# The opening of a graph layer and attention kernel: two elements' first products placed together, with loads and VectorE's order rearranged

## The chip, the cores and the metric

The kernel runs on one NeuronCore of one Trainium2 chip. The metric is device time in microseconds (us). A NeuronCore has TensorE (PE in the profile; PEld is its weight load), VectorE (DVE), ScalarE (ACT), GpSimd (POOL) and SyncE (SP), whose queue here issues the transfers between the chip's large memory (HBM) and the on-chip memory (SBUF). Products of TensorE land in a third memory, PSUM, of which this kernel uses eight banks of 128 x 512 numbers.

## The reference

The input x has 64 elements of 256 x 512 numbers (256 graph nodes with 512 features); adj is one 256 x 256 graph of zeros and ones. All arithmetic is in 32-bit floats. Two layers follow each other, each with a residual addition and a layer normalization over the features:

```python
a = adj.astype(x.dtype)
deg = a.sum(axis=1)
mi, mj = x @ Wi.T, x @ Wj.T                      # W = [Wi | Wj], 512 x 1024
h = layernorm(x + deg * (mi + b) + a @ mj)       # per element, layer 0
q, k, v = h @ Wq.T + bq, h @ Wk.T + bk, h @ Wv.T + bv   # 8 heads of 64
p = softmax(where(adj == 0, -inf, q @ k.T / 8))
out = layernorm(h + (p @ v) @ Wo.T + bo)         # layer 1
```

## The kernel before

The elements are worked through in pairs, 32 passes. In the steady loop (line 982 on) layer 0 of the next pair is woven between the attention of the present pair. Before the loop stands an opening, written out by hand, which brings the weights and the first two elements in, runs layer 0 for both, and then the first projections.

Layer 0 of an element takes seven block products instead of eight, with sums of blocks on both sides. `xB` is a loaded element, in an order that VectorE turns by one transpose into `xT` (`turn_x`, line 488). The left sums `S1` to `S4` of `xT` go to `xS` (`sum_x`, line 494). On the weights' side `w0` holds seven blocks: three come straight from memory (B11 and B21 of Wi, B22 of Wj), and T1 to T4 are made from them by `combine` (line 923), where T3's place first receives the raw B12 of Wj. Steps 1 to 7 of `l0_steps` (line 502) are the products, each two matmuls of 128 x 128 by 128 x 512:

- step1 is x times B11, into the bank "x"; ScalarE copies it out as the keeper `u1`. step3 adds x times B21 to the same bank.
- step2 is x times T4, into the bank "w"; the result goes, scaled by the degree, into the residual `xh`.
- step4 (S2 with T2) and step6 (S3 with T3) share the bank "y"; after step4 VectorE writes the keeper `u2` = y + `u1`, after step6 `u3` = y + `u1`.
- step5 (S1 with T1) and step7 (S4 with B22) share the bank "z". `mj`'s second half is z after step5 plus `u3` (added on GpSimd); its first half is z after step7 plus `u2`.
- each half of `mj` is split into `hi` (ScalarE) and `lo` (GpSimd). Step 8, `neighbours`, multiplies the graph with both. Steps 9 to 14 normalize the rows (`take`, `give`) and, in the loop, send them on.

In the lists `p` (element 0) and `q` (element 1) these steps are counted from 0: `p[0]` is step1, `p[7]` is `neighbours`, `p[12]` is the normalization of the first row block.

What sets the order. A planner in the language places the instructions and all waits. TensorE's instructions, and those of other engines that are wrapped in `in_order` (line 282), are pinned behind the instruction that was written before them on the same engine. The others may move when their inputs are there. SyncE issues transfers in the order of the profile's issue lines. A tile of a pool has as many buffers as the pool says per tag: the banks of layer 0 and of the projections (`bank`, tag "mm") are three, the value bank (`value_bank`) is one, the keepers (tag "lu") are three, and tiles in `p1` have one. A tile that finds no buffer waits until an earlier one has been read for the last time.

In the opening before, SyncE issues the first x, then B11, the raw B12, adj, B21, B22, the first residual and the biases; the second x follows when the transpose of the first has freed its only buffer. The products are run in the order of lines 940 and 945, then `make_factors` (line 412) makes right-hand sums of the attention weights, `h_transpose` turns element 0's rows for the projections, and line 962 starts these.

Of the kernel before, what the change touches and what calls it, by code (L numbers as in the profile page):

```python
# [8 lines left out]
F32 = mybir.dt.float32  # L9
# [7 lines left out]
P = 128  # L17
# [201 lines left out]
B11, B21, B22, T1, T2, T3, T4 = range(7)  # L219
# [5 lines left out]
def unshifted_path(ctx, tc, flag, x, adj, wiT, wjT, b0, wqT, bq, wkT, bk, wvT, bv, woT, bo, out):  # L225
# [16 lines left out]
    nc = tc.nc  # L242
    B, N, D = x.shape
# [3 lines left out]
    R = 32  # L247
# [9 lines left out]
    p1 = ctx.enter_context(tc.tile_pool(name="p1", bufs=1))  # L257
# [11 lines left out]
    def bank(name):  # L269
        return ps_m.tile([P, 512], F32, tag="mm", name=name)  # L270
# [27 lines left out]
    def load_x(b):  # L298
        if b < B:
            xh[b] = p6.tile([P, NT, D], F32, tag="xh", name="xh")  # L300
            nc.sync.dma_start(out=xh[b], in_=x[b].rearrange("(t p) d -> p t d", p=P))

    b_bc = p4.tile([P, D], F32, tag="u", name="b_bc")
    xB, hB = {}, {}

    def load_xB(b):
        if b < B:
            xB[b] = p1.tile([P, N // R, P], F32, tag="xB", name="xB")
            for q in range(D // P):
                nc.sync.dma_start(out=xB[b][q * R:(q + 1) * R],  # L310
                                  in_=x[b][:, q * P:(q + 1) * P].rearrange("(r a) n -> r a n", r=R))

    load_xB(0)
    w0 = const.tile([P, 7, 2, D], F32, name="w0")
    adj_i = p2.tile([P, NT, N], I32, tag="pe", name="adj_i")
    for n, w, h in ((B11, wiT, 0), (T3, wjT, 0), (None, None, 0), (B21, wiT, 1), (B22, wjT, 1)):
        if n is None:
            nc.sync.dma_start(out=adj_i, in_=adj.rearrange("(t p) j -> p t j", p=P))
        else:
            nc.sync.dma_start(out=w0[:, n], in_=w.rearrange("(p h c) o -> p h c o", h=2, c=2)[:, h])  # L320
    load_x(0)
    nc.sync.dma_start(out=b_bc, in_=b0.to_broadcast([P, D]))

    xT, xS, hT, hS, qT, kT, vv, aoT, oS = ({} for _ in range(9))

# [20 lines left out]
    def degrees():  # L346
        in_order(nc.vector.tensor_copy(a, adj_i))
        in_order(nc.vector.tensor_reduce(deg, a, AX.X, ALU.add))

    def turn_graph():  # L350
        for t in range(NT):
            pt = score_bank("pt_a")[:, :N]
            for i in range(NT):
                transpose(pt[:, i * P:(i + 1) * P], a[:, i, t * P:(t + 1) * P], ident)

            in_order(nc.vector.tensor_copy(graph[:, t, :], pt))
            in_order(nc.scalar.copy(aT[:, t, :], pt))
# [28 lines left out]
    def bias_steps():  # L386
        for t, d in ((bq_sb, bqd), (bk_sb, bkd)):
            in_order(nc.vector.tensor_sub(d, t[:, 2:4], t[:, 0:2]))
# [83 lines left out]
    def left_blocks(a11, a12, a21, a22, s):  # L472
        return {"A11": a11, "A12": a12, "A21": a21, "A22": a22,
                "S1": s[:, 0], "S2": s[:, 1], "S3": s[:, 2], "S4": s[:, 3]}
# [13 lines left out]
    def turn_x(b, tag="xT"):  # L488
        if b < B:
            xT[b] = p1.tile([P, NC, N], F32, tag=tag, name="xT")  # L490
            transposed(xT[b], xB.pop(b))
            load_xB(b + 1)

    def sum_x(b):
        if b < B:
            a11, a12, a21, a22 = (xT[b][:, 2 * k:2 * k + 2, t * P:(t + 1) * P]
                                  for t in range(NT) for k in range(2))
            xS[b] = left_blocks(a11, a12, a21, a22, p1.tile([P, 4, 2, P], F32, tag="xS", name="xS"))
            for step in left_steps(xS[b], in_order):
                step()  # L500

    def l0_steps(b):
        banks, k = {}, {}

        def product(name, left, n, first):
            if first:
                banks[name] = bank("po")
            for c in range(2):
                matmul(banks[name], left[:, c, :], w0[:, n, c, :], start=(first and c == 0),
                                 stop=(c == 1), skip_group_check=True)  # L510

        def raw(t, h):
            return xT[b][:, 2 * h:2 * h + 2, t * P:(t + 1) * P]

        def keeper(name):
            k[name] = p3.tile([P, D], F32, tag="lu", name=name)
            return k[name]

        def add_scaled(t, src):
            nc.vector.scalar_tensor_tensor(xh[b][:, t, :], src, deg[:, t:t + 1], xh[b][:, t, :],  # L520
                                           ALU.mult, ALU.add)

        def split(t):
            nc.scalar.copy(k["hi"][:, t, :], k["mj"][:, t, :])
            nc.gpsimd.tensor_tensor(k["lo"][:, t, :], k["mj"][:, t, :], k["hi"][:, t, :].bitcast(F32),
                                    ALU.subtract)

        def step1():
            product("x", raw(0, 0), B11, True)
            nc.scalar.copy(keeper("u1"), banks["x"])  # L530

        def step2():
            product("w", raw(1, 1), T4, True)
            add_scaled(1, banks["w"])

        def step3():
            product("x", raw(0, 1), B21, False)
            add_scaled(0, banks["x"])

        def step4():  # L540
            product("y", xS[b]["S2"], T2, True)
            nc.vector.tensor_add(keeper("u2"), banks["y"], k["u1"])

        def step5():
            product("z", xS[b]["S1"], T1, True)
            k["mj"] = p1.tile([P, NT, D], F32, tag="mj", name="mj")
            nc.scalar.copy(k["mj"][:, 1, :], banks["z"])  # L547

        def step6():
            product("y", xS[b]["S3"], T3, False)  # L550
            nc.vector.tensor_add(keeper("u3"), banks["y"], k["u1"])
            nc.gpsimd.tensor_tensor(k["mj"][:, 1, :], k["mj"][:, 1, :], k["u3"], ALU.add)

            k["hi"] = p1.tile([P, NT, D], F32R, tag="hi", name="hi")
            k["lo"] = p1.tile([P, NT, D], F32R, tag="lo", name="lo")
            split(1)
            add_scaled(1, k["u3"])

        def step7():
            product("z", xS[b]["S4"], B22, False)  # L560
            nc.vector.tensor_add(k["mj"][:, 0, :], banks["z"], k["u2"])
            split(0)

        stats = {}

        def neighbours():
            k["pa"] = score_banks("pa")
            for i in (1, 0):
                for n, (j, part) in enumerate((j, part) for j in (1, 0) for part in ("hi", "lo")):
                    matmul(k["pa"][:, i, :], graph[:, j, i * P:(i + 1) * P], k[part][:, j, :],  # L570
                           start=(n == 0), stop=(n == 2 * NT - 1))

        def take(t):
            r = xh[b][:, t, :]
            in_order(nc.vector.tensor_add(r, k["pa"][:, t, :], r))
            stats[t] = norm_stats(r, in_order)

        def give(t):
            norm_apply(xh[b][:, t, :], *stats[t], in_order)


        return [step1, step2, step3, step4, step5, step6, step7, neighbours, lambda: take(1), lambda: take(0),
                lambda: give(1), lambda: send_h(b, 1), lambda: give(0), lambda: send_h(b, 0)]
# [30 lines left out]
    def h_transpose(b, t, borrow=False):  # L614

        g, i = divmod(b, NB)
        if i == 0 and t == 1:
            new_h(g)
        pt = (score_banks("pt_h")[:, 0, :] if borrow else bank("pt_h")).rearrange("p (c n) -> p c n", c=NC)
        for c in range(NC):  # L620
            transpose(pt[:, c, :], xh[b][:, t, :].rearrange("p (n c) -> p c n", c=NC)[:, c, :], ident)
        nc.scalar.copy(hT[g][:, :, i * N + t * P:i * N + (t + 1) * P], pt)
        if t == 0 and i == NB - 1:
            sum_h(g)
# [284 lines left out]
    def run(steps):  # L909
        for s in steps:  # L910
            s()
# [12 lines left out]
        in_order(nc.vector.tensor_sub(w0[:, n], w0[:, m], w0[:, k]))  # L924

    turn_x(0)
    load_x(1)
    raw_q, raw_k = load_raw(wqT, "kT"), load_raw(wkT, "oS")
    load_x(2)
    raw_v, raw_o = load_raw(wvT, "v"), load_raw(woT, "aoT")  # L930
    for _ in range(6):
        bring()
    sum_x(0)
    combine(T1, T3, B11)
    degrees()
    combine(T2, B22, T1)
    combine(T4, B21, T2)
    combine(T3, B22, T3)
    p, q = l0_steps(0), l0_steps(1)
    run([p[0], p[2], p[4], p[3]])  # L940
    turn_x(1, "hB")
    degree_bias()
    add_bias(0)
    turn_graph()
    run([p[1], p[5], q[0], p[6], q[2]])
    add_bias(1)
    sum_x(1)
    run(q[1:2] + p[7:11] + q[3:5] + p[12:13])
    make_factors(wqT, "wq", raw_q)
    for _ in range(AHEAD - 6):  # L950
        bring()
    bias_steps()
    h_transpose(0, 1)
    run(q[5:6])
    h_transpose(0, 0)
    run(q[6:7])
    make_factors(wkT, "wk", raw_k)
    o = second_late(qk_steps(0, qT, "qT", bq_sb, bqd, True))
    k = second_late(qk_steps(0, kT, "kT", bk_sb, bkd, True))
# [22 lines left out]
    for g in range(NG - 1):  # L982
# [15 lines left out]
        w = NB * NC - 2  # L998
# [3 lines left out]
        o = o_steps(g)  # L1002
# [111 lines left out]
```

## Time and profile before

| | us |
|---|---|
| median of 4 runs | 3116.52 |
| lowest and highest | 3114.95 and 3118.49 |
| the profiled execution | 3119.08 |
| its span, first to last instruction | 3117.2 |
| TensorE busy in the span | 3073.8 |
| VectorE busy | 2148.9 |
| GpSimd busy | 1521.8 |
| ScalarE busy | 1008.3 |

A row of the profile gives a source line, an engine, an operation with the tile that it writes and the ones that it reads, their shapes, a count and durations. In the timeline a row begins with the start and the length in us; the brackets at its end give how long the engine had been idle and what ended the wait. One matmul of 32-bit floats is recorded as two, so that a product of layer 0 is four records. Line 290 is the helper through which all matmuls go; the tile names tell them apart: `po` from `w` and `xT` or `xS` is layer 0, `pa` the neighbours, `pt_h` a transpose of rows, `st` a projection. SPq is SyncE's issuing queue. A DMA issue line gives the KB of one and the us from issue to landing.

### The profile page before, as it was taken

Reading aid. Unit: us, or ns where it says so; the run is one execution under the profiler, and the core shown is the slowest. Engines: PE = TensorE matmul, PEld = TensorE weight load, DVE = VectorE, ACT = ScalarE, POOL = GpSimd, SP = SyncE. Lnnn points to the kernel's source line nnn. Section 1 sums busy time; section 2 is a strip of 40 time slices with the busy share of each in tenths; the row PEclk is TensorE's granted clock in tenths of the full one; section 3 lists DMA queues with packets and bytes.
Section 4 is the critical chain, followed back from the end, with each engine's and each line's share of the span. In section 5 each row is a group of like instructions: output and inputs, shape, how many; then the busy total and the mean of one; then the engine's idle time right before and its main releaser. Section 6 shows DMA issues by size and latency. Waiting matters only on the chain. (4 is left out here: it accounts for less than half of the span.)

```text
span 3117.2 us, 42777 instructions
## 1 busy us (share of the span) xinstructions
PE 3073.8 (99%) x14598; PEld 2118.4 (68%) x14598; DVE 2148.9 (69%) x3234; ACT 1008.3 (32%) x1925; POOL 1521.8 (49%) x1255
## 2 busy tenths in 40 slices
PE   7999999999999999999999999999999999999998
PEld 4667766677666777666776667766677766677665
DVE  6766676766677666676667676667766767767665
ACT  2332333323333333333233333333333333323332
POOL 2544545544545445464454544455544546445453
PEclk9999999999999999999999999999999999999999
DMA  7355534455444554445553445544455444555333
GB/s 245 123 151 157 166 118 133 132 157 165 140 123 126 155 168 149 117 128 154 158 157 123 132 136 157 165 136 125 127 154 169 145 120 126 155 162 160 116 113 96
DMA packets 410395, 447.28 MB, mean 143 GB/s; under 512 B 40896, under 2 KB 300224, under 8 KB 409792
## 3 DMA queue, kind: packets, MB, share of 16 engines
q1 hardware_dynamic: 410176, 444.50, 48.1%
q8 instruction: 120, 1.97, 0.3%
q14 instruction: 99, 0.81, 0.1%
HBM read 340.79 MB, written 70.25 MB: 132 GB/s over the span
## 5 line engine op out<-in xcount | busy, mean ns | idle before, releaser
L461 POOL TENSOR_TENSOR rstd<-ve,mhalf 128x1 f32<-128x1 f32 x256 | 140.8, 555 | 725.9 <-DVE below L459 725.9
L812 POOL TENSOR_TENSOR pk<-pe 128x512 f32<-128x512 f32 x256 | 322.2, 1275 | 340.7 <-ACT pe L809 340.6
L290 PE MATMUL po<-w,xS 128*128 128x512 f32 x1024 | 470.9, 602 | 6.1 <-ACT mj L547 5.7
L290 PE MATMUL st<-hS,factor 128*128 128x256 f32 x2048 | 452.7, 379 | 1.2 <-DVE u L685 1.2
L290 PEld LDWEIGHTS st<-hS,factor 128*128 128x128 f32 x2048 | 388.2, 190 | 55.3 <-DVE u L685 1.6
L809 ACT ACTIVATE pe<-pe 128x1024 f32<-128x1024 f32 x256 | 270.8, 1058 | 379.2 <-DVE pe L805 379.2
L290 PE MATMUL st<-hT,factor 128*128 128x256 f32 x1536 | 360.7, 381 | 9.1 <-ACT u L711 8.4
L290 PE MATMUL po<-w,xT 128*128 128x512 f32 x768 | 354.3, 604 | 14.7 <-DVE xS L478 9.4
L290 PEld LDWEIGHTS po<-w,xS 128*128 128x128 f32 x1024 | 187.2, 190 | 253.0 <-issue 191.6
L290 PEld LDWEIGHTS st<-hT,factor 128*128 128x128 f32 x1536 | 289.0, 190 | 61.6 <-ACT u L711 20.9
L805 DVE TENSOR_TENSOR pe<-ps,maskT 128x1024 f32<-128x1024 f32 x256 | 297.8, 1194 | 35.2 <-PE ps L290 35.2
L882 DVE RECIPROCAL rden<-den 128x256 f32<-128x256 f32 x127 | 222.9, 1755 | 74.0 <-PE den L290 68.5
L290 PEld LDWEIGHTS po<-w,xT 128*128 128x128 f32 x768 | 144.2, 192 | 183.1 <-issue 163.6
L290 PE MATMUL ps<-qT,kT 64*128 64x256 f32 x2048 | 264.9, 392 | 0.0
L883 POOL TENSOR_TENSOR rtot<-rtot,rden 128x256 f32<-128x256 f32 x127 | 92.7, 730 | 330.1 <-DVE rden L882 330.1
L290 PE MATMUL pav<-pe,v_sb 128*64 128x256 f32 x2048 | 250.1, 386 | 1.9 <-ACT pe L809 1.8
L740 DVE TENSOR_TENSOR xh<-st,xh 128x512 f32<-128x512 f32 x186 | 144.6, 777 | 151.5 <-PE st L290 151.5
L290 PEld LDWEIGHTS pav<-pe,v_sb 128*64 128x64 f32 x2048 | 135.2, 136 | 154.1 <-issue 71.9
L290 PEld LDWEIGHTS ps<-qT,kT 64*128 64x128 f32 x2048 | 184.3, 186 | 78.2 <-issue 51.3
L290 PE MATMUL st<-factor,hS 128*128 128x256 f32 x1024 | 234.8, 382 | 0.0
L290 PE MATMUL st<-factor,oS 128*128 128x256 f32 x992 | 224.2, 379 | 0.0
L290 PEld LDWEIGHTS st<-factor,hS 128*128 128x128 f32 x1024 | 191.9, 190 | 35.4 <-issue 10.6
(115 smaller groups left out, 4658.2 us busy)
## 6 DMA issues: line engine op xcount, KB each, us to landing
xB<-in_x_dram SPq DMA_DIRECT2D x256, 128.0 KB, 3.7
xh<-in_x_dram SPq DMA_DIRECT2D x64, 512.0 KB, 4.5
factor<-wq SPq DMA_DIRECT2D x128, 256.0 KB, 4.3
factor<-wk SPq DMA_DIRECT2D x128, 256.0 KB, 2.6
factor<-wv SPq DMA_DIRECT2D x128, 256.0 KB, 2.6
spread<-rden SPq DMA_DIRECT2D x1016, 32.0 KB, 1.9
factor<-wo SPq DMA_DIRECT2D x124, 256.0 KB, 3.1
h_cols<-xh SPq DMA_DIRECT2D x124, 256.0 KB, 2.4
```

The lines of the kernel that those rows point to most:

```text
L290: in_order(nc.tensor.matmul(*args, **kw))
L461: nc.gpsimd.tensor_tensor(rstd, ve, mhalf, ALU.pow)
L740: nc.vector.tensor_add(dst, src, dst)
L805: nc.vector.tensor_add(pe.rearrange("p j t q -> p j (t q)"), ps.rearrange("p j t q -> p j (t q)"), maskT.rearrange("p t q -> p (t q)").uns ...
L809: in_order(nc.scalar.activation(flat, flat, AF.Exp, scale=QSCALE, accum_out=etot[:, NB * g + i, pr:pr + 1]))
L812: nc.gpsimd.tensor_tensor(pk, pe[:, :, 0, :], pe[:, :, 1, :], ALU.add)
L882: nc.vector.reciprocal(rden, den)
L883: nc.gpsimd.tensor_tensor(rtot, rtot, rden, ALU.add)
```

## The change

The second element's x is loaded at the start, into the buffer tagged "hS", which is idle in the opening, and the other loads are put in another order: B11, B21, the second x, adj, the raw B12, B22, the bias, the two residuals. The third x is issued right behind the second transpose in the program, ahead of the raw attention weights. VectorE sums the first x right after its transpose, then turns the second, and only then takes the graph and combines the weights. The sums of the second x go to the buffer tagged "qT" instead of "xS", so that they need not wait for the first's. TensorE runs the two products by B11 and B21 of element 0, then those of element 1, and then the products by combined weights; element 1's bank "x" is the value bank. The second bias addition is placed after element 0's statistics, and each `h_transpose` stands behind a product of element 1 instead of before it.

```diff
-    def load_xB(b):
+    def load_xB(b, tag="xB"):
         if b < B:
-            xB[b] = p1.tile([P, N // R, P], F32, tag="xB", name="xB")
+            xB[b] = p1.tile([P, N // R, P], F32, tag=tag, name="xB")
...
-    for n, w, h in ((B11, wiT, 0), (T3, wjT, 0), (None, None, 0), (B21, wiT, 1), (B22, wjT, 1)):
-        if n is None:
-            nc.sync.dma_start(out=adj_i, in_=adj.rearrange("(t p) j -> p t j", p=P))
-        else:
-            nc.sync.dma_start(out=w0[:, n], in_=w.rearrange("(p h c) o -> p h c o", h=2, c=2)[:, h])
+    def load_w0(n, w, h):
+        nc.sync.dma_start(out=w0[:, n], in_=w.rearrange("(p h c) o -> p h c o", h=2, c=2)[:, h])
+
+    load_w0(B11, wiT, 0)
+    load_w0(B21, wiT, 1)
+    load_xB(1, "hS")
+    nc.sync.dma_start(out=adj_i, in_=adj.rearrange("(t p) j -> p t j", p=P))
+    load_w0(T3, wjT, 0)
+    load_w0(B22, wjT, 1)
+    nc.sync.dma_start(out=b_bc, in_=b0.to_broadcast([P, D]))
     load_x(0)
-    nc.sync.dma_start(out=b_bc, in_=b0.to_broadcast([P, D]))
+    load_x(1)
...
             transposed(xT[b], xB.pop(b))
-            load_xB(b + 1)
-
-    def sum_x(b):
+            if b > 0:
+                load_xB(b + 1)
+
+    def sum_x(b, tag="xS"):
...
-    def l0_steps(b):
+    def l0_steps(b, bank_of_x=bank):
...
             if first:
-                banks[name] = bank("po")
+                banks[name] = (bank_of_x if name == "x" else bank)("po")
...
     turn_x(0)
-    load_x(1)
+    sum_x(0)
+    turn_x(1, "hB")
     raw_q, raw_k = load_raw(wqT, "kT"), load_raw(wkT, "oS")
     load_x(2)
     raw_v, raw_o = load_raw(wvT, "v"), load_raw(woT, "aoT")
     for _ in range(6):
         bring()
-    sum_x(0)
+    degrees()
     combine(T1, T3, B11)
-    degrees()
     combine(T2, B22, T1)
     combine(T4, B21, T2)
     combine(T3, B22, T3)
-    p, q = l0_steps(0), l0_steps(1)
-    run([p[0], p[2], p[4], p[3]])
-    turn_x(1, "hB")
+    p, q = l0_steps(0), l0_steps(1, value_bank)
+    run([p[0], p[2], q[0], q[2], p[4], p[3]])
+    turn_graph()
+    sum_x(1, "qT")
     degree_bias()
     add_bias(0)
-    turn_graph()
-    run([p[1], p[5], q[0], p[6], q[2]])
+    run([p[1], p[5], p[6], q[1], q[3]])
+    run(p[7:11] + [q[4]])
     add_bias(1)
-    sum_x(1)
-    run(q[1:2] + p[7:11] + q[3:5] + p[12:13])
+    run([p[12]])
     make_factors(wqT, "wq", raw_q)
     for _ in range(AHEAD - 6):
         bring()
     bias_steps()
+    run(q[5:6])
     h_transpose(0, 1)
-    run(q[5:6])
+    run(q[6:7])
     h_transpose(0, 0)
-    run(q[6:7])
     make_factors(wkT, "wk", raw_k)
```

More of the change, by code (lines that the diff above doesn't have):

```diff
@@ L497, in sum_x @@
                                   for t in range(NT) for k in range(2))
-            xS[b] = left_blocks(a11, a12, a21, a22, p1.tile([P, 4, 2, P], F32, tag="xS", name="xS"))
+            xS[b] = left_blocks(a11, a12, a21, a22, p1.tile([P, 4, 2, P], F32, tag=tag, name="xS"))
             for step in left_steps(xS[b], in_order):
                 step()
-    def l0_steps(b):
+    def l0_steps(b, bank_of_x=bank):
         banks, k = {}, {}
```

## The prediction

> **What bounds the kernel now.** I read the page first, then busy time by stretch, TensorE's timeline of the opening, the granted clock, the load issues with their time to landing, and the waits of SyncE's queue.
>
> ```profile
> PE 3073.8 (99%) x14598; PEld 2118.4 (68%) x14598; DVE 2148.9 (69%) x3234; ACT 1008.3 (32%) x1925; POOL 1521.8 (49%) x1255
> ```
>
> TensorE (PE) is busy nearly throughout: 43.4 us idle in 3117.2. By stretch (PE is the number after the length):
>
> ```profile
> 0.00:60.00 60.00, 43.71 (x120) 23.29 (x121) 37.73 (x59) 13.13 (x25) 16.06 (x20) 0.97 0.80 261
> ...
> 130.00:3000.00 2870.00, 2856.36 (x13634) 1979.40 (x13632) 1986.41 (x2985) 938.54 (x1794) 1420.35 (x1165) 1.00 0.48 143
> ```
>
> So 16.3 of the idle lie in the first 60 us, where the change is; 13.6 are spread over the middle. What TensorE saves before its first attention product therefore reaches the end, if nothing late takes its place. Its opening (start, length, then in brackets the idle time before):
>
> ```profile
> 9.38 3.75 PE L290 MATMUL po<-w,xT 128*128 128x512 f32 x4 [9.38 <-DVE xS L478]
> 14.45 3.75 PE L290 MATMUL po<-w,xT 128*128 128x512 f32 x4 [1.32 <-DMA w<-in_wiT_dram]
> ...
> 28.50 3.57 PE L290 MATMUL po<-w,xT 128*128 128x512 f32 x4 [2.77 <-DVE xT L485]
> ...
> 39.64 3.70 PE L290 MATMUL po<-w,xS 128*128 128x512 f32 x8 [0.44 <-DVE xS L478]
> 44.51 0.75 PE L293 MATMUL pt_h<-ident,xh 128*128 128x128 f32 x4 [1.17 <-ACT xh L467]
> ...
> 48.18 0.75 PE L293 MATMUL pt_h<-ident,xh 128*128 128x128 f32 x4 [1.21 <-ACT xh L467]
> ...
> 50.49 1.89 PE L290 MATMUL st<-hT,factor 128*128 128x256 f32 x8
> ```
>
> A product of layer 0 is four records. Up to about 18.5 they start 0.86 apart (3.44 a product), later 0.43 (1.72): half clock, though the clock column has no record before 18.5. Halved again here:
>
> ```profile
> 28.80:32.10 3.30, 3.30 (x5) 1.24 (x4) 2.04 (x3) 0.70 (x2) 2.94 (x2) 0.50 1.03 423
> ```
>
> Ledger of 9.38 to 50.49, 41.1 us: idle 1.32 + 2.77 + 0.44 + 1.17 + 1.21 = 6.9; half clock over 3.75 + 4.05 (14.45 to 18.5) + 3.4 = 11.2 busy us, of which half, 5.6, is loss; work at full clock 28.6. Avoidable at most: 12.5. The start at 9.38 is B11's landing (issued 3.47, 5.8 later), not the VectorE line that the view names. Loads, by issue, with time to landing:
>
> ```profile
> w<-in_wiT_dram SPq DMA_DIRECT2D x1, 512.0 KB, 5.8
> ...
> w<-in_wjT_dram SPq DMA_DIRECT2D x1, 512.0 KB, 8.2
> ...
> adj_i<-in_adj_dram SPq DMA_DIRECT2D x1, 256.0 KB, 8.4
> ...
> w<-in_wiT_dram SPq DMA_DIRECT2D x1, 512.0 KB, 9.3
> ```
>
> They land at 9.3, 12.3, 13.0, 14.4. SyncE also stalls:
>
> ```profile
> SPq L392 <- DMA w<-in_wjT_dram: 2.4, 1, 2.4
> ...
> SPq L310 <- DMA w<-in_wiT_dram: 1.0, 1, 1.0
> ```
>
> In both the issue waits for the load eight places ahead: eight are in flight at most.
>
> **What the Trainium skill says.** "TensorE: Matmul & The Clock Gate", Part 1: the clock starts at half and is granted after a busy window of 3.4 us, windows running freely. The trace agrees: changes at 18.5, 28.8, 32.2. "PSUM — Partial Sum Buffer", PSUM bank collisions: two engines may not use one bank at once, so a copy out must finish before the next matmul into it; no run here shows a collision. "SBUF — State Buffer", Who interferes with whom: VectorE and GpSimd share a port pair under an exclusive lock. The trace agrees: a sum (L478) took 2.50 us beside a GpSimd bias addition, 0.42 elsewhere.
>
> **The change, part by part.** p and q are the steps of elements 0 and 1, numbered from 0.
>
> Loads. B11 stays second, so PE starts at 9.4 again. B21 takes T3's place: 12.3. Then by bytes at the 364 GB/s of 9.4 to 15.1 us (0.5 MB in 1.44): second x 13.8, adj 14.5, T3 16.0, B22 17.4, b0 18.1, xh0 19.5, xh1 21.0. The second x is in rows of 512 B, costlier: 13.3 to 15.5. The eight-deep limit costs nothing there: B22's issue waits for B11 (9.3), the bias for B21 (12.3), when earlier loads are still moving. xB2's four issues now stand before the raw weights on SyncE; the last waits for xh1, about 21, against 20.3 for the first raw weight now. Then 0.5 MB more goes ahead: raw weights 2 to 3 us later, the first factor at about 38 instead of 36.4, needed at 45. Hidden by 7 us; without that cover, 2.
>
> VectorE. Second transpose 13.8 to 15.9 (2.06); adjacency cast and degrees 1.11: 17.0; T1, T2, T4, T3 at 1.21 each: 18.2, 19.4, 20.7, 21.9. They are wanted on PE at about 20.8, 22.5, 24.8, 26.5. Hidden, with 2.5 us spare.
>
> PE. Removed: 1.32, 2.77, 0.44, 1.17, 1.21 and the second half-clock stretch. The last two waits go because two second-element products and a finished normalization now stand between. Added:
> - p0 to p2 share a bank, and the copy u1 (0.59, 13.17 to 13.76) must come between: 0.70. Today B21's landing hides it. B21 at 12.3 is in time.
> - q0 to q2 likewise; today p6 lies between. 0.59, hand-over 0.1, and 0.17 of overlap lost: 0.87.
> - The keepers "lu" have three buffers. q's u1 takes one early; u1 and u2 of p hold the others. p's u3 (p5) must wait until u2 is released, by the addition behind p6. PSUM follows: q1's bank is the fourth of three. The x bank of p has passed to p1, whose addition into xh0 waits for the first bias addition (GpSimd, 2.35, not over before 31). So q1 waits for the addition behind p6: 0.95 (bounds 0 and 1.5).
> - u3 late makes GpSimd late: bias addition to about 31.6, then 1.28 for mj, 0.62 on ScalarE, 1.27 each for two lo parts: 35.5. PE reaches the neighbours' product at 34.2: 1.3 (bounds 0 and 2.5).
> - The last transpose now stands directly before the first q product: the copy of hT (0.59) is bare, 0.75. Today a product of 1.88 covers it.
>
> Sum of idle 4.6. Half clock: from 9.38 with a gap of 0.7; if the window ending at 15.1 counts as busy, 5.05 us at half, loss 2.5; if not, until 18.5, 8.4 us, loss 4.2. (Today's window there, 62% busy, did not count; this one would be 80%.) New total 7.1 or 8.8 against 12.5: saving 5.4 or 3.7, 4.6 in the middle. The steps after 50 keep their order: unchanged. xh1's bias addition is moved behind the statistics of element 0 on GpSimd; behind it waits only q5's addition into xh1: nothing.
>
> Against the profiled execution (3119.1; span 3117.2, 1.9 around it) this gives 3114.5. That execution lies 2.6 above the median; the second half-clock stretch (1.7) needs a window that catches most of the 2.77 idle, and I estimate that a run in four or two lacks it. Against the median, 3116.5, I take 4.2: **3112.3**.
>
> **The rivals.**
> *Fuller gain* (0.20): neither the slot nor GpSimd is late: 0.95 + 1.3 more, 3110, with the clock early 3108.5. For it: GpSimd is 16 us busy in 60. Against: u3's buffer is counted, not estimated.
> *Late loads eat it* (0.15): second x after 16. VectorE's whole order stands behind its transpose; each us is one of PE and keeps the clock low. 3 us late gives about 3116. For it: slow rows of 512 B. Against: the first x, with the same rows, was in use at 6.4.
> *Slower* (0.13): the remaining order is planned afresh, and in each of the 31 later passes one wait grows, most likely VectorE behind GpSimd's lock. Today a pass idles 13.6/31 = 0.44 us. From 0.14 us a pass the gain is gone, from 0.35 it is slower by over 0.2%: at 0.4, 3124.7. For it: 2.50 for 0.42 shows what one lock costs. Against: PE's order is written out, and at 69% VectorE has room.
> That the change does not do what it says: a small part of the second rival.
>
> **How the numbers follow.** The forecast has 0.52, its own range 3110 to 3115. 0.2% is 6.2 us, about what a measurement of this kernel can tell from no change: 3110.3 and 3122.7 are the borders. Faster: most of the fuller gain and a small part of the forecast, 0.25. Slower: 0.15, the rival and some of what I have not seen. Same: 0.60. Range for 8 in 10: 3108 to 3118, which takes in the fuller gain and late loads and leaves out the slower case.
>
> **What would show it.** First product at 9.4; B21's product 0.7 after u1's copy; second transpose over by 16.5; q0 without a wait; u3 of p after the addition behind p6; a wait of about 1 before q1 and of about 1 before the neighbours' product; first q product at 44 to 46 instead of 50.49; middle idle 13 to 14 us. Wrong if the second x lands after 16, if the clock stays half beyond 18.5, or if the middle's idle moves by over 4.

## The result, and the profile after

The changed kernel has a median of 3119.66 us against 3116.92 for the kernel before: 2.7 us more. The measured ratio is 1.0011 with a 95% interval of 1.0006 to 1.0016 (the medians alone give 1.0009). That is inside the 0.2% of the forecast "same", but it lies on the other side of no change than the 3112.3 that was predicted, and outside the range of 3108 to 3118. The profiled execution took 3118.74 us.

What lies after the opening did not change. Busy time by stretch, changed kernel (start and end, length, then busy time of each engine, PE first):

```profile
0.00:60.00 60.00, 42.84 (x122) 23.31 (x123) 39.89 (x60) 13.00 (x25) 17.05 (x20) 0.97 0.82 264
...
130.00:3000.00 2870.00, 2856.54 (x13636) 1979.67 (x13630) 1986.87 (x2986) 938.71 (x1794) 1420.38 (x1164) 1.00 0.48 143
```

The middle idles 13.5 us, as before (13.6), so what changed lies in the opening. This execution took 0.3 us less than the profiled one of the kernel before (3119.08), although the median is 2.7 more: that one was slow in its opening, as its second execution shows further down. Its waits can be compared line by line; its total can't stand for the median. The opening on TensorE, changed kernel:

```profile
8.39 3.71 PE L290 MATMUL po<-w,xT 128*128 128x512 f32 x4 [8.39 <-DVE xS L482]
12.77 1.98 PE L290 MATMUL po<-w,xT 128*128 128x512 f32 x4 [0.68 <-ACT u L536]
15.21 1.98 PE L290 MATMUL po<-w,xT 128*128 128x512 f32 x4 [0.45 <-DVE xT L490]
17.87 1.98 PE L290 MATMUL po<-w,xT 128*128 128x512 f32 x4 [0.68 <-ACT u L536]
...
30.27 1.98 PE L290 MATMUL po<-w,xT 128*128 128x512 f32 x4 [1.40 <-DVE xh L526]
32.09 1.88 PE L290 MATMUL po<-w,xS 128*128 128x512 f32 x4
35.19 0.49 PE L290 MATMUL pa<-hi,graph 128*128 128x512 f32 x1 [1.22 <-ACT hi L530]
36.54 0.50 PE L290 MATMUL pa<-lo,graph 128*128 128x512 f32 x1 [0.85 <-POOL lo L531]
...
42.15 0.75 PE L293 MATMUL pt_h<-ident,xh 128*128 128x128 f32 x4 [0.29 <-ACT xh L472]
...
44.46 0.68 PE L293 MATMUL pt_h<-ident,xh 128*128 128x128 f32 x4
48.34 7.13 PE L290 MATMUL st<-hT,factor 128*128 128x256 f32 x24 [3.21 <-ACT hT L628]
```

Of the five waits that were to go, the one for B21, the one for element 1's sums and the one before the last transpose are gone; 0.45 of the 2.77 for the second transpose of x is left (none in a second execution, below), and 0.29 of the 1.17 before the first transpose of rows. The last transpose starts at 44.46, when nothing but the first q product is left to start; before, that product started at 50.49 (47.40 in the second execution). Then TensorE stands still for 3.21 us until ScalarE has copied the transposed rows, and the clock is taken down behind the wait:

```profile
49.60:52.80 3.20, 3.20 (x9) 2.57 (x8) 3.17 (x5) 1.36 (x3) 1.29 (x1) 0.50 0.90 273
```

That costs about another 1.7 us: the eight records of the q product that start from 49.58 to 52.57 are 0.43 apart, the others 0.22. Why the copy is late can be read from two queues. ScalarE, changed kernel:

```profile
44.24 0.56 ACT L628 COPY hT<-pt_h 128x512 f32<-128x512 f32 x1
47.19 0.62 ACT L530 CAST hi<-mj 128x512 fp32r<-128x512 f32 x1 [2.38 <-POOL mj L558]
47.71 0.58 ACT L628 COPY hT<-pt_h 128x512 f32<-128x512 f32 x1
```

The second copy of hT stands behind `hi` of element 1, and `hi` waits 2.38 us for GpSimd's `mj`. GpSimd, changed kernel:

```profile
42.16 0.99 POOL L466 TENSOR_TENSOR rstd<-ve,mhalf 128x1 f32<-128x1 f32 x1 [1.24 <-DVE below L464]
43.13 2.36 POOL L379 TENSOR_TENSOR xh<-xh,degb 128x1024 f32<-128x1024 f32 x1
45.44 1.71 POOL L558 TENSOR_TENSOR mj<-mj,u 128x512 f32<-128x512 f32 x1
```

The second bias addition (L379) stands behind element 0's statistics, where the change put it. It takes 2.36 us, and `mj` waits behind it. The chain of the loss is then: bias addition, `mj`, `hi`, copy of hT, first q product. (VectorE's sums for the weights, 0.68 alone, took 2.77 and 1.74 beside these two GpSimd instructions. VectorE is not in this chain: the keeper that `mj` adds was written by 43.34.)

### The profile page after: what moved, and what is told of

Read it like the earlier page. It is cut to its first block, busy times and chain, and to the rows that moved or that the text cites. A ratio compares the mean times of both kernels' runs of the same rounds, so it can differ in the third digit from the quotient of the medians.

```text
span 3116.8 us, 42774 instructions
## 1 busy us (share of the span) xinstructions
PE 3072.6 (99%) x14598; PEld 2118.2 (68%) x14598; DVE 2151.0 (69%) x3234; ACT 1008.1 (32%) x1925; POOL 1522.5 (49%) x1255
## 5 line engine op out<-in xcount | busy, mean ns | idle before, releaser
L290 PE MATMUL po<-w,xT 128*128 128x512 f32 x768 | 351.3, 600 | 12.8 <-DVE xS L482 8.4
```

Of the source, the lines that this page charges most:

```text
L290: in_order(nc.tensor.matmul(*args, **kw))
```

## The experiments

Theory A: this chain is the loss, and the added place of the bias addition is its cause. Theory B: the loss lies elsewhere, in the loads, the clock at the start or the shared banks. All medians below are compared with the kernel before on the same chip (3117.0 in the first group, 3116.2 in the second, 3117.1 in the third), and "over before" is the difference; brackets give the ratio and its 95% interval.

**The bias addition earlier, or later.** In the traces of both, the order on VectorE and ScalarE is that of the changed kernel, as far as operations and tile names tell; on GpSimd one instruction stands elsewhere.

```diff
     run([p[1], p[5], p[6], q[1], q[3]])
+    add_bias(1)                       # bias_early
     run(p[7:11] + [q[4]])
-    add_bias(1)
...
     h_transpose(0, 0)
+    add_bias(1)                       # bias_late, instead
```

> Changed kernel, with the second bias addition moved ahead of element 0's statistics; only GpSimd's order differs. Theory A (the addition stands before element 1's mj on GpSimd, so hi is late, and hi stands before the last copy of hT on ScalarE): the wait before the first q product falls from 3.2 to under 1 us and the clock is not lowered behind it, so 2.3 + 1.7 = 4 us less than the changed kernel, 3115.7, ratio to before 0.9996. Theory B (the loss lies elsewhere, in loads or in the clock at the start): within 1 us of the changed kernel, 3119 to 3120.

> Changed kernel, with the second bias addition moved behind element 1's last layer-0 product. Theory A: as with the early place, about 4 us less than the changed kernel, 3115.7; GpSimd then adds the bias after both lo parts, when nothing waits for it. Theory B: 3119 to 3120.

Measured: 3116.94 (0.1 under before, ratio 1.0, 0.9991 to 1.0008) and 3116.75 (0.3 under before, the same interval). So 2.7 and 2.9 us of the changed kernel go with one instruction's place in a queue, that is, the whole of its loss. (Its interval, from 1.0006, and theirs, to 1.0008, just touch, but two places of the instruction give the same, and the traces show why.) The wait, early place, then ScalarE there:

```profile
47.15 3.72 PE L290 MATMUL st<-hT,factor 128*128 128x256 f32 x16 [1.13 <-ACT hT L628]
```

```profile
45.12 0.56 ACT L628 COPY hT<-pt_h 128x512 f32<-128x512 f32 x1
45.99 0.62 ACT L530 CAST hi<-mj 128x512 fp32r<-128x512 f32 x1 [0.30 <-POOL mj L558]
46.51 0.58 ACT L628 COPY hT<-pt_h 128x512 f32<-128x512 f32 x1
```

And with the late place:

```profile
49.16 3.72 PE L290 MATMUL st<-hT,factor 128*128 128x256 f32 x16 [1.13 <-ACT hT L628]
```

The wait falls from 3.21 to 1.13, and that of `hi` from 2.38 to 0.30. Theory A holds for the loss against the kernel before; B is out, since loads and banks are as in the changed kernel. The gain is smaller than the 4 expected. In the profile of either kernel the clock is lowered after all, now at the neighbours' product (early place, its records 0.43 apart instead of 0.23):

```profile
35.90:39.10 3.20, 3.14 (x7) 2.48 (x8) 0.00 (x0) 0.00 (x0) 2.33 (x2) 0.50 0.81 260
```

The waits there, 1.22 and 0.85, are those of the changed kernel, so the move did not lengthen them. Why the clock falls behind them in one execution and not in another is worked out in the last section.

**The transposes back ahead of element 1's products.** The bias addition stays late; this asks whether ScalarE's order alone can mend it.

```diff
-    run(q[5:6])
     h_transpose(0, 1)
-    run(q[6:7])
+    run(q[5:6])
     h_transpose(0, 0)
+    run(q[6:7])
```

> Changed kernel, with the two transposes of rows put back ahead of element 1's last two products; the bias addition stays late. Theory A: ScalarE copies hT ahead of hi, so the first q product waits for nothing, but the first transpose waits about 2 us for its normalization: first q product at about 46.8 instead of 48.3, and 1.7 of clock, 3 us less, 3116.7. A rival within A (GpSimd alone counts, not ScalarE's order): no gain, 3119 to 3120.

Measured: 3118.62, 1.6 over before (1.0006, 0.9998 to 1.0014). That is about 1 us less than the changed kernel, within the intervals, and 1.9 more than theory A expected. The wait of 3.2 is gone, as theory A says, but the wait that this order has by itself took its place, with a lowered clock (43.8 to 47.0):

```profile
43.70 1.13 PE L293 MATMUL pt_h<-ident,xh 128*128 128x128 f32 x4 [2.01 <-ACT xh L472]
...
49.78 3.40 PE L290 MATMUL st<-hT,factor 128*128 128x256 f32 x15
```

(This execution also waited 1.56 us, until 16.75, for the second transpose of x, against 0.45 in the changed kernel's.) By the waits the change's order of the transposes is the better one once the addition is out of the way: 0.29 and 1.13 us in the kernels above against 2.01 here. The two orders were not run against each other with the addition moved.

**The wait filled with idle matmuls**, to price the clock by itself. The three matmuls are additional, and nothing reads their results.

```diff
     h_transpose(0, 0)
+    spare = score_bank("spare")
+    for _ in range(3):
+        matmul(spare, xT[1][:, 0, 0:P], w0[:, B11, 0, :], start=True, stop=True)
```

> Changed kernel with three more matmuls of 128x128 by 128x512 (2.6 us, into a spare bank, results unused) between the last transpose and the first q product; they fill the wait of 3.2 us. If the lowered clock behind the wait costs 1.7 us: first q product still at 48.3, its matmuls 0.22 apart at once, 3118.0. If the clock costs nothing or the wait doesn't set it: 3119.7 or more.

Measured: 3118.45, 1.4 over before (1.0005, 0.9997 to 1.0014): 1.3 less than the changed kernel by the difference to before, for 1.7 expected. The first q product started at 49.08, 40.0 us after the first product, as in the changed kernel (48.34 and 8.39). In its profile the clock stays full from 12.0 us to the end of the work. The interval reaches to the changed kernel's ratio, so the size is only rough; that the clock is lost behind the wait, and kept when the wait is filled, is what the traces show.

**u3's missing buffer.** The prediction had named it as the cause of the waits at q1 and at the neighbours' product. The second bias addition is in its late place.

```diff
-            k[name] = p3.tile([P, D], F32, tag="lu", name=name)
+            k[name] = p4.tile([P, D], F32, tag="lu", name=name)
...
-        pool, tag = (p3, "lu") if early and name == "u1" else (p4, "u")
+        pool, tag = (p4, "lu") if early and name == "u1" else (p4, "u")
```

> The kernel with the second bias addition moved behind element 1's last product (3116.8), and four keepers of tag lu instead of three. If u3's missing buffer costs what its waits show (1.40 before q1, about 2.1 before and in the neighbours' product, and the lowered clock that they bring): 3 us less, 3113.7, ratio to before 0.9989, no wait before q1. If GpSimd's chain alone sets the neighbours' product: only 1.4 less, 3115.4.

Measured: 3113.32, 2.9 under before (0.999, 0.9981 to 0.9998), 2.7 less than the late bias addition alone by the same measure. No wait before q1, and little in the neighbours' product:

```profile
28.76 1.88 PE L290 MATMUL po<-w,xT 128*128 128x512 f32 x4
...
32.79 0.50 PE L290 MATMUL pa<-lo,graph 128*128 128x512 f32 x1 [0.20 <-POOL lo L531]
...
34.02 0.50 PE L290 MATMUL pa<-lo,graph 128*128 128x512 f32 x1 [0.50 <-POOL lo L531]
```

Of 3.47 us of waits at these two places 0.70 are left, and the clock is full from 13.0 on. The missing buffer is shown as the cause of these waits; how many of the 2.7 us are theirs is rough, since the two intervals overlap.

**The first bias addition later**, with three keepers and the second addition in its late place, since the trace ends q1's wait with the addition into xh0.

```diff
-    add_bias(0)
-    run([p[1], p[5], p[6], q[1], q[3]])
+    run([p[1], p[5], p[6]])
+    add_bias(0)
+    run([q[1], q[3]])
```

> As above with three keepers, but the first bias addition is moved behind element 0's last product in the program, so that on GpSimd and on the bank of p1 nothing waits for it. If q1 waits for that bank (the trace ends the wait with the addition into xh0): no wait before q1, 1.4 less, and some of the wait in the neighbours' product, 3114.6. If u3's buffer is what q1 waits for: no change at q1, 3116.8.

Measured: 3118.10, 1.9 over before (1.0004, 0.9995 to 1.0012), where 3114.6 was expected. The wait before q1 is gone, so the bank of p1 was its nearer cause. But GpSimd now does the addition between `mj` and the second `lo`, and the neighbours' product waits 1.68 and 2.37 us:

```profile
31.78 1.72 POOL L558 TENSOR_TENSOR mj<-mj,u 128x512 f32<-128x512 f32 x1
33.46 2.35 POOL L379 TENSOR_TENSOR xh<-xh,degb 128x1024 f32<-128x1024 f32 x1
35.77 1.26 POOL L531 TENSOR_TENSOR lo<-mj,hi 128x512 fp32r<-128x512 f32 x1
```

It is the same fault as the change's own: the addition was moved past work, and the work behind it on GpSimd was what TensorE waited for next.

**Loads and VectorE's order alone**, with the products as before.

```diff
-    run([p[0], p[2], q[0], q[2], p[4], p[3]])
+    run([p[0], p[2], p[4], p[3]])
...
+    run([p[1], p[5], q[0], p[6], q[2]])
+    add_bias(1)
+    sum_x(1, "qT")
+    run(q[1:2] + p[7:11] + q[3:5] + p[12:13])
```

> The changed kernel's loads, buffers and VectorE order with the products, transposes and bias additions in the order of before. The wait of 2.8 before element 1's first product goes, but the first product by combined weights (p4) now waits for the second transpose and the graph, about 2.8, since nothing of element 1 stands ahead of it. Theory: 3116.5, as before (within 1.5). Rival: the early second x is the gain by itself, 3113.

Measured: 3115.59, 0.7 under before (0.9999, 0.999 to 1.0007): the same as before by this measurement. Its profiled execution, 3113.83, is the fastest of its 13. In it the wait of 2.77 before element 1's first product has fallen to 0.91 (for a bank, ended by the addition into xh) and the lowered clock with it; the waits of 1.17 and 1.21 before the transposes are unchanged, and u1's copy is bare (0.68). Its p4 waited 0.42 and not 2.8, but in a run whose second product still ran at half clock, so that part is not settled.

**Toward a faster opening.** With both bias additions late, four keepers, element 1's second product behind p4 and the value-bias product in the last gap (lines as in the edits above, and what goes from the old places, are left out):

```diff
-    run([p[0], p[2], q[0], q[2], p[4], p[3]])
+    run([p[0], p[2], q[0], p[4], q[2], p[3]])
...
     bias_steps()
+    spread_value_bias()
...
     h_transpose(0, 0)
+    fold_value_bias(raw_o)
```

> The changed kernel with both bias additions late, four keepers, element 1's second product behind p4 (u1's copy is hidden), and the product that folds the value bias moved into the gap behind the last transpose. By the waits that go (1.40, 2.1, 0.68, 1.13) and the lowered clock: 3111.5, ratio 0.9983. If each wait only moves on to the next product: 3115 or more.

Measured: 3116.39, as before (1.0, 0.9991 to 1.0008), 5 us more than expected. Two waits took the place of the ones removed: the first transpose waits 1.22 us, since the statistics now stand behind the first bias addition, and the value-bias product waits 2.73 for a copy (`spread`) that was placed too late on VectorE:

```profile
45.77 0.41 DVE L429 COPY spread<-bv_t 128x512 f32<-128x512 f32 x1
...
46.28 3.67 PE L290 MATMUL pb<-raw,spread 128*128 128x512 f32 x8 [2.73 <-issue]
```

So I went back to the first bias addition in its old place, and added the other parts one by one: the covered copy of u1 (`hid`), then the value-bias product, placed as in `best`, with its copy ahead of the weight sums (`best2`).

```diff
     run([p[12]])
+    spread_value_bias()               # best2
     make_factors(wqT, "wq", raw_q)
```

> The kernel with the late second bias addition and four keepers (3113.3), with element 1's second product moved behind p4, so that the copy of u1 is covered. If the gap of 0.68 (0.87 with the lost overlap) was on the path: 3112.6. If the later waits only grow by it: 3113.3.

> The same, and the product that folds the value bias moved into the gap behind the last transpose, with the copy that it reads made early on VectorE. The gap there, 1.13, closes: 3111.6. If that copy or the raw weights come late as they did before (2.7 of wait): 3114.

Measured: 3113.07, 4.0 under before (0.9987, 0.9981 to 0.9994), and 3112.52, 4.6 under before (0.9986, 0.9979 to 0.9992). By their intervals both are faster than the kernel before, by a little over 0.1%, and so than the changed kernel. The steps from 2.9 to 4.0 and 4.6 go the expected way, but are smaller than the intervals, so how much each of the two parts brings stays open. In the profile of `best2` the last gap is closed:

```profile
42.35 0.63 PE L293 MATMUL pt_h<-ident,xh 128*128 128x128 f32 x4
42.82 3.60 PE L290 MATMUL pb<-raw,spread 128*128 128x512 f32 x8
46.26 5.34 PE L290 MATMUL st<-hT,factor 128*128 128x256 f32 x24
```

**Both kernels profiled once more**, to see how far one profiled execution stands for the median.

> The kernel before, unchanged, profiled once more. If its first profiled execution (3119.1, against a median of 3116.9) was slow in the opening: first q product near 48.3 instead of 50.49, with less half clock. If the difference lies after the opening: near 50.5 again.

> The changed kernel, unchanged, profiled once more. Its first profiled execution (3118.7) lies below its median (3119.7). The wait before the first q product, 3.2, and the two around the neighbours' product should come back within 0.2; the places of lowered clock should move, since they did between the kernels.

The kernel before, second execution, 3116.97 us, almost its median:

```profile
8.06 3.78 PE L290 MATMUL po<-w,xT 128*128 128x512 f32 x4 [8.06 <-DVE xT L485]
13.37 1.96 PE L290 MATMUL po<-w,xT 128*128 128x512 f32 x4 [1.53 <-DMA w<-in_wiT_dram]
...
25.41 3.28 PE L290 MATMUL po<-w,xT 128*128 128x512 f32 x4 [2.77 <-DVE xT L485]
...
47.40 5.34 PE L290 MATMUL st<-hT,factor 128*128 128x256 f32 x24
```

The first q product starts at 47.40 and not at 50.49. The waits are the same within about 0.2; the start is 1.3 earlier, and the clock is full from 12.3 instead of 18.5. The lowered clock behind the wait of 2.77 is there again (26.1 to 29.3). The changed kernel, second execution, 3119.80 us, begins its first q product at 49.65 behind a wait of 3.20, and the clock falls behind it (50.7) as in the first.

## Why the prediction was wrong

**First step that failed: the sentence on xh1's bias addition, "behind it waits only q5's addition into xh1: nothing".** It listed what waits for the addition's result, not what is queued behind it on GpSimd. There stood element 1's `mj`, behind that `hi` on ScalarE, and behind `hi` the copy of hT. The prediction had the copy of hT as 0.75; it was 3.21, and 1.13 with the addition moved away. Behind the wait the clock was lost for another 1.7. By the medians the place of this one addition is worth 2.7 to 2.9 us.

**Second: the base.** The ledger of 12.5 us was taken from an execution whose opening was slow by 3.1 us against one near the median. The same ledger on the second execution gives 1.53 + 2.77 + 0.44 + 1.17 + 1.21 = 7.1 of idle and half of 3.78 + 3.4, 3.6: 10.7. I allowed 0.4 of the 2.6 between execution and median, and took it from the wrong place: the lowered clock behind 2.77 is in both executions, what differs is the start and when the clock is first full.

**Third: sizes, and what released q1.** Before q1 the wait was 1.40 for 0.95, and it did not end with the addition behind p6. VectorE, changed kernel:

```profile
29.47 0.75 DVE L526 SCALAR_TENSOR_TENSOR xh<-po,deg,xh 128x512 f32<-128x512 f32 x1 [2.47 <-POOL xh L379]
30.14 0.68 DVE L567 TENSOR_TENSOR mj<-po,u 128x512 f32<-128x512 f32 x1
30.85 0.69 DVE L557 TENSOR_TENSOR u<-po,u 128x512 f32<-128x512 f32 x1
```

q1 began at 30.27, when the addition into xh0 (L526, which had waited for GpSimd's first bias addition) was over and the one behind p6 (L567) was not: it took p1's bank, and in `both_late`, where that addition was early, the wait is gone. With four keepers u3 (L557) was written at 27.24, and q1 began at 28.76, before the addition into xh0 (29.53) and the one behind p6 (31.19). Of the three banks only the one that u3 reads had been read out by then. So the missing buffer was rightly named, but it acted through that bank. In the neighbours' product, 1.22 + 0.85 = 2.07 for 1.3; the keeper's missing buffer, named as the cause, was it. The two gaps for u1's copy were 0.68 each for 0.70 and 0.87, the gap before the first transpose 0.29 for 0. u3 came after the addition behind p6, as said. Whether a window with a gap of 0.7 counts as busy at the start was left open, and it falls either way: a window with 0.67 us idle was followed by the full clock in `late_lu4`, and not in `bias_late`, `loads_only`, `best` and the changed kernel's second execution.

The sum on the second executions, both near their medians. Changed kernel: idle 0.68 + 0.68 + 1.40 + 2.07 + 0.29 + 3.20 = 8.3; half of 3.75 + 3.5 busy us until 16.6, 3.6; behind the last wait 1.7: 13.6. Kernel before: 10.7. The difference, 2.9, with a start that was 0.6 later in this execution, makes 3.5 against a measured 2.8 (3119.80 less 3116.97); the other 0.7 stay open. With the predicted 0.75 in place of 3.20 and no clock lost behind it, the sum would be 9.4, 1.3 less than before: even then the gain would have been a third of the 4.2 that was forecast.

Of the 7.4 us between the forecast of 3112.3 and 3119.66, the addition's place thus accounts for 2.7 to 2.9, the base for about 1.4 (12.5 less 10.7, less the 0.4 allowed), and the sizes for about 1.7 (0.45 + 0.77 + 0.29 + 0.38 for the copy of hT that remains, less 0.2). This sum is an estimate from the traces above, and some 1.5 us are in none of the three. That "same" came true is no success of the account: a gain of 4.2 was argued, and a loss of 2.7 happened to fall inside the same 0.2%.

**What held.** The first product started at B11's landing (8.4 to 8.7). B21 was in time: its product followed u1's copy by 0.05. The second transpose ended at 15.2 (16.5 was the limit), and the weight sums at 20.9 (21.9). The eight-deep issue limit and the later raw weights cost nothing that the trace shows. The middle idles as before: the rival that made the kernel slower through the later passes fell. The rival of late loads is not the loss, but there is something in it. In the profiles of other kernels here with the same loads, TensorE waited up to 1.31 (`best2`) and 1.56 us (`ht_first`) for the second transpose of x, so that its limit holds in some executions only. The rows of 512 B can be seen in the kernel before: from 14 to 16 us, with the second x among what moved, its DMA engines moved 312 GB/s, from 12.8 to 14 they had moved 410, equally busy (1.05 and 1.04). The loss came from inside the opening, by a chain that no rival contained.

## What to carry to other kernels

When an instruction is moved in a queue, follow the queue and not only its result: list what now stands behind it on its engine, then what stands behind each of those on theirs, until a chain meets the engine that bounds the kernel. Where a change of a few us is judged from a trace, take the ledger from an execution near the median, or from two. A gap that is opened on the bounding engine is priced with the clock that may be lost behind it. It can be filled with work that has to be done anyway, as the value-bias product fills it in `best2`, if that work's own inputs are there: in `best` the same product waited 2.73 us.

## What the runs showed of the hardware

What takes the clock down can be read from the clock records of the fourteen profiles. But for the one at the end of the kernel, each stretch of lowered clock lasts 3.41 us, and the stretches of full clock between are whole multiples of that (10.24 in the kernel before, three; 37.55 in the changed kernel, eleven). So the changes of one execution lie on one grid of windows, and the grid lies elsewhere in each execution. Over all windows from the first full clock on, the clock was lowered after every one in which TensorE idled 1.87 us or more, and after none in which it idled 1.78 or less (idle by the profile, which models the ends of matmuls). Some of them:

| window (us) | idle in it | clock after it |
|---|---|---|
| kernel before, 25.34 to 28.75 | 2.77 | half |
| changed kernel, 46.05 to 49.47 | 2.29 | half |
| `ht_first`, 40.31 to 43.72 | 2.00 | half |
| `bias_early`, 32.35 to 35.77 | 1.87 | half |
| `best`, 41.91 to 45.32 | 1.76 | full |
| changed kernel, 32.40 to 35.82 | 1.34 | full |

So the length of a wait alone does not decide it. The 2.73 of `best` were split between two windows, 1.76 and 0.96. The 1.22 and 0.85 at the neighbours' product fell mostly into one window with the moved bias additions, and not in either profile of the changed kernel. From these figures, as an estimate: a wait of 2.77 is split so evenly that neither part reaches 1.8 in about one execution of four. The Trainium skill ("TensorE: Matmul & The Clock Gate", Part 1) has the windows running freely; these observations agree with that, and the 3.41 with its window.

- The first full clock came between 11.9 and 18.5 us over these profiles, with the first matmul between 8.0 and 9.4. In one execution of the changed kernel it was granted at 11.9, in the other at 16.6; the second product then took 1.98 us in the one and ran at half clock, 3.5 us, in the other.
- The same load takes different times from one execution to the next. B21, loaded second, landed 6.4 and 6.2 us after its issue in the two executions of the changed kernel and 7.5 in `ht_first`; the second load of the kernel before, of the same size, 8.2 and 7.0.
